# Edge tables by node made on ACT from destination rows, zero fills issued side by side, and a planner with other numbers, in a graph attention and mixture-of-experts kernel

## The chip, the cores and the metric

The kernel runs on one core of one Trainium2 chip. The metric is the device time in microseconds (us) of one launch; lower is better. Engines: PE multiplies matrices, DVE (vector), ACT (scalar, activation functions) and POOL (GpSimd, which here issues indirect gathers and scatters) work beside it, and SP issues the plain DMAs. Each engine takes its instructions in the order in which the program gives them.

## The reference, cut to what matters

6250 nodes of 256 values, 100,000 edges sorted by destination. A graph attention layer with eight heads, a feed-forward net per node, then a mixture of eight experts of which each node takes two.

```python
h = (xn @ W).reshape(N, HEADS, HEAD_DIM)
e = leaky_relu(a_src[src] + a_dst[dst], 0.2)
ee = exp(e - segment_max(e, dst)[dst])
alpha = ee / segment_sum(ee, dst)[dst]
agg = segment_sum(h[src] * alpha[:, :, None], dst)
out = layer_norm(agg + xn @ W_res + bias)
x = x + out + gelu_tanh(out @ ffn_w1 + ffn_b1) @ ffn_w2 + ffn_b2
...
logits = layernorm(x) @ Wr + br          # then softmax, the top two experts
x = x + sum of the two experts' weight * (gelu(xn_e @ W1[e] + b1[e]) @ W2[e] + b2[e])
```

## The kernel before

**Setup** (to L761) makes the products of all nodes, writes a table `tab_s` of node rows (256 values of h and 16 source factors) to DRAM, a table `tab_q` of the 16 destination factors per node, and from the edges' destination indices the columns `loct` (which of the 32 nodes of its window an edge belongs to) and `snloc` (which of 128 accumulator rows a window's node stands for).

**Edges.** The edges lie in 784 tiles of 128. Four windows of 32 nodes make a group; a group has m = 1, 2, 4 or 8 tiles per window, so the four windows' i-th tiles make one *edge step*. There are 110 groups (66 with m = 1) and 196 steps, taken from the highest nodes down, so the first 66 steps end a group each. The stages of a step run at different delays in iterations of the main loop:

```python
STAGES = ((sum_up, 6), (weigh, 3), (add_tiles, 4), (place, 4), (turn_spread, 1), (give, 2),
          (spread, 0), (add_nodes, 5), (fetch, 0))
```

- `fetch` (L824, POOL): four indirect gathers of `tab_s` rows into `gs` (four buffers).
- `spread` (L833, DVE): the table `oh` of edges by node, one where an edge (its partition) belongs to a node (32 columns per window). At a group's first step it also makes `qd` (L840, DVE): the destination factors `gd` of the four windows' nodes, multiplied with the mask `quad`, so that each window's factors stand in columns of their own and zeros beside them. `gd` is loaded for 32 groups at once (L808, SP).
- `turn_spread` (L846, PE): transposes `oh` into the PSUM tile `pt`; ACT copies it out as `oht` (L848), now nodes on partitions and edges in columns. The tile `pt` has one buffer and also serves the transposes of `turn` (L978, evicted by ACT at L985).
- `give` (L854, PE): `oht` times `qd` brings each edge its destination factors, `pz`.
- `weigh` (L862 to L866, DVE): the edges' weights, then the weighted rows `msg`.
- `add_tiles` (L881, PE): `oh` times `msg` sums the edges by node in `pl`; behind a group's last step ACT copies it out as `part` (L885).
- `place` (L899, DVE, once a group): `oh2`, the table that puts the window nodes at their accumulator rows.
- `add_nodes` (L906, PE) and `sum_up` (L917, DVE, twice): add the group into `acc_hi` or `acc_lo`.

**Everything else is tasks.** A *first unit* (25 of them) makes `xn @ W_res` plus biases and stores it; a *node unit* (25, two tiles of nodes each, the last a single tile) takes the summed edges, norms them, runs the feed-forward net, stores the new rows (`store_new`, L1106, SP) and chooses the experts; every two node units a *chunk* ranks their nodes per expert, and POOL scatters their rows into the experts' lists `xs` (L1396). A *block* (53, three of them half) loads 256 rows of one expert's list (`xb`, L1456) and its weights (`w1b`, `w2b`, `b2b`, L1447 to L1449, 2.2 MB), runs the expert's net (`turn` L978, `up` L993 with the eviction `ht` at L996, `down` L1003) and adds the result to the output by an indirect scatter (L1498, POOL). A node unit may start once the edges of its nodes are summed; a block once enough chunks are listed. Before the last chunk, `clear` (L1408, SP) writes 384 rows of zeros behind the end of each of the eight experts' lists, because the last blocks may be only partly filled.

**The order** is fixed when the program is built: each iteration of the main loop first emits the stages of the edge steps, then takes tasks from a list in order, as far as each engine's budget (in the planner's own cost units) and the tasks' dependences allow:

```python
ROOM = {"PE": 7.5, "DVE": 7.6, "ACT": 5.0, "POOL": 2.6, "SP": 1e9}
EDGES = {"PE": 1.3, "DVE": 2.0}
BEHIND = {"PE": 0.5, "DVE": 1.4}
ROOM_AFTER = {"PE": 7.7, "DVE": 7.0, "ACT": 7.0, "POOL": 5.2, "SP": 1e9}
```

`EDGES` is taken off for each step and `BEHIND` for one that ends a group; `ROOM_AFTER` holds once the edge steps are done. A task of another engine comes at least one iteration behind what it needs unless a gap is given. `turn_of` is the order of the blocks; the half blocks have the numbers 50 to 52.

Of the kernel before, what the change touches and what calls it, by code (L numbers as in the profile page):

```python
# [48 lines left out]
ALU = mybir.AluOpType  # L50
# [18 lines left out]
EDGES = {"PE": 1.3, "DVE": 2.0}  # L69
BEHIND = {"PE": 0.5, "DVE": 1.4}  # L70
ROOM_AFTER = {"PE": 7.7, "DVE": 7.0, "ACT": 7.0, "POOL": 5.2, "SP": 1e9}
# [151 lines left out]
def gnn_moe_kernel(  # L223
# [68 lines left out]
    NCW = -(-NW // P)  # L292
    DUMMY = NP
# [12 lines left out]
    for i in range(NS - NF):  # L306
        turn_of += [NF + i, NF - (NS - NF) + i]
# [23 lines left out]
    xt_d = dp.tile([NT, P, KD * P], F32, name="xt_d")  # L331
    xs = dp.tile([E * CAP + BT, DX], F32, name="xs")
# [13 lines left out]
    snloc = gp.tile([P, NQ], F32, name="snloc")  # L346
    here = gp.tile([P, 2, NQ], F32, name="here")
# [55 lines left out]

    quad = cp.tile([P, G], F32, name="quad")
    nc.vector.memset(quad, 0.0)
    for j in range(G):
        nc.vector.memset(quad[j * W32:(j + 1) * W32, j:j + 1], 1.0)
# [52 lines left out]
    with ExitStack() as actx:  # L460
# [96 lines left out]
        nc.vector.tensor_copy(srf, srow)  # L557
        ends = ap_.tile([P, 2, NCH], F32, name="ends")
# [69 lines left out]
        for j in range(G):  # L628
            q = slice(j * W32, (j + 1) * W32)
            nc.vector.tensor_scalar(sn[q], first[q, :, j], pcol[q], float(-j * W32), op0=ALU.add,  # L630
                                    op1=ALU.add)
        nc.vector.tensor_sub(sn, sn, kff)
        nc.vector.tensor_scalar(snloc, sn, float(P), float(-P), op0=ALU.is_ge, op1=ALU.mult)
        nc.vector.tensor_add(snloc, snloc, sn)
        nc.vector.tensor_sub(sn, first[:, :, 0], kff)
# [45 lines left out]

        nc.vector.memset(acc_hi[:, NT - KHI, :], 0.0)
# [100 lines left out]
    GC = P // G  # L783
# [13 lines left out]
    gds = {}  # L797

    def fetch_nodes(c):

        gq = bw.tile([P, W32 * 2 * H], F32, name="gq", bufs=1)
        nc.gpsimd.indirect_dma_start(
            out=gq, out_offset=None, in_=tab_q,
            in_offset=bass.IndirectOffsetOnAxis(ap=qrow[:, c:c + 1], axis=0))
        nc.sync.dma_start(tab_g[c * P:(c + 1) * P, :], gq)
        n = min(GC, NQ - c * GC)
        gd = bw.tile([P, GC, 2 * H], F32, name="gd")
        nc.sync.dma_start(gd[:, :n], tab_g[c * P:c * P + n * G, :].rearrange(  # L808
            "(g j) (r c) -> (j r) g c", j=G, r=W32))
        gds[c] = gd  # L810
# [18 lines left out]
    def spread(s):  # L829

        q, i = order[s]
        oh = bw.tile([P, G, W32], F32, name="oh", bufs=6)
        nc.vector.tensor_tensor(oh, jrow[:, None, :W32].to_broadcast([P, G, W32]),  # L833
                                step_tiles(s, loct)[:, :, None].to_broadcast([P, G, W32]),
                                op=ALU.is_equal)
        live[s, "oh"] = oh
        if i == 0:
            qd = bw.tile([P, G, 2 * H], F32, name="qd", bufs=3)
            gd = gds[q // GC][:, q % GC, :]
            nc.vector.tensor_tensor(qd, gd[:, None, :].to_broadcast([P, G, 2 * H]),  # L840
                                    quad[:, :, None].to_broadcast([P, G, 2 * H]), op=ALU.mult)
            live[q, "qd"] = qd

    def turn_spread(s):
        po = cps.tile([P, KD, 2 * P], F32, name="pt")
        nc.tensor.transpose(po[:, 0, :P], live[s, "oh"].rearrange("p j r -> p (j r)"), ident)  # L846
        oht = bw.tile([P, P], F32, name="oht")
        nc.scalar.activation(oht, po[:, 0, :P], AF.Copy)  # L848
        live[s, "oht"] = oht

    def give(s):

        pz = bps.tile([P, G * 2 * H], F32, name="pz", bufs=2)
        nc.tensor.matmul(pz, live.pop((s, "oht")), live[order[s][0], "qd"].rearrange(  # L854
            "p j c -> p (j c)"), start=True, stop=True)
        live[s, "pz"] = pz
# [38 lines left out]
    @behind_group  # L895
    def place(q):

        oh2 = bw.tile([P, P], F32, name="oh2")
        nc.vector.tensor_scalar(oh2, jrow[:, :P], snloc[:, q:q + 1], None, op0=ALU.is_equal)  # L899
        live[q, "oh2"] = oh2  # L900
# [9 lines left out]
    def sum_up(q):  # L910
# [4 lines left out]
        for b in range(2):  # L915
# [6 lines left out]
    STAGES = ((sum_up, 6), (weigh, 3), (add_tiles, 4), (place, 4), (turn_spread, 1), (give, 2),  # L922
              (spread, 0), (add_nodes, 5), (fetch, 0))
# [17 lines left out]
    pending = []  # L941
    held = set()

    def task(*a, **k):
        t = Task(*a, **k)
        pending.append(t)
        return t
# [243 lines left out]
    loads, turned, added, normed, chosen_, scattered = [], [], [], [], [], []  # L1191

    def node_unit(u):
        t0, n, _ = units[u]
        env = {"n": n}
        ld = task(lambda: load_nodes(t0, n, env), "SP", 0.0,
                  [(firsts[u], 0),
                   *[(d, 0) for d in back(turned, 2) + back(added, 2) + back(normed, 3)]])
        dv = task(lambda: divide(t0, n, env), "DVE", 0.85 * n, [ld])
# [17 lines left out]
        loads.append(ld)  # L1217
# [171 lines left out]
    placed = {u: [] for u in range(NT)}  # L1389
    between = cp.tile([P, 1], F32, name="between")  # L1390

    def scatter(u, j):
        t = units[u][0] + j
        n = rows(t)
        for k in range(2):
            st = nc.gpsimd.indirect_dma_start(  # L1396
                out=xs, out_offset=bass.IndirectOffsetOnAxis(ap=slots[k][:n, t:t + 1], axis=0),
                in_=xes[u // 2][:n, place_of(u) + j, :], in_offset=None)
            tc.add_to_no_dep_group("slots", st.ins)
            placed[u].append(st.ins)  # L1400
            tc.declare_no_dep(st.ins, group="slots", reason="each token has slots of its own")

            nc.gpsimd.memset(between, 0.0)

    def clear(e):

        r = nc.sync.value_load(endi[0:1, e:e + 1], min_val=0, max_val=E * CAP - 3 * P)
        nc.sync.dma_start(xs[bass.ds(r, 3 * P), :].rearrange("(p r) d -> p r d", r=3),  # L1408
                          blank[:, None, :].to_broadcast([P, 3, DX]))

    def chunk_tasks(us, final, before_final):
# [17 lines left out]
        for u in us:  # L1429
            scattered.append([task(lambda u=u, j=j: scatter(u, j), "POOL", 2.6,  # L1430
                                   [rk, ad, *[(d, 0) for d in cleared]])
                              for j in range(units[u][1])])
            sc += scattered[-1]
# [116 lines left out]
    EARLY = 10  # L1550
    final_list, there = [], None
    s, u, since, was_nodes = 0, 0, [], False

    with tc.manual_schedule():
        nc.sync.dma_start(xs[E * CAP:, :].rearrange("(p r) d -> p r d", r=2),
                          blank[:, None, :].to_broadcast([P, 2, DX]))
        while s < NG + LASTST or pending or u < len(units) or len(blocks) < NS:
            for g in range(s, min(s + EARLY, NG)):
                if order[g][0] // GC not in gds:
                    fetch_nodes(order[g][0] // GC)  # L1560
# [19 lines left out]
            while sum(t.cost for t in pending if t.eng == "PE") < QUEUE:  # L1580
                if (u < len(units) and units[u][2] <= s - LASTST
                        and not (ahead and was_nodes)):
                    was_nodes = True
                    node_unit(u)
                    since.append(u)
                    u += 1
                    if u % 2 == 0 or u == len(units):
                        chunk_tasks(since, u == len(units), u == len(units) - 1)
                        since = []
                elif ahead:  # L1590
# [55 lines left out]
```

## Time and profile before

| | us |
|---|---|
| median of 3 runs (lowest, highest) | 1924.65 (1918.36, 1925.77) |
| the profiled execution | 1919.82 |
| its span | 1917.9 |
| edge steps, first and last transpose of L846 | 122.1 to 1580.6 |
| first and last product of the experts' second layer finished (L1488) | 680.9 to 1903.4 |
| gathers of L824, 784 of them, mean of one | 1.041 |
| ACT table loads at L996, 41 of them, mean of one | 1.283 |

The page divides the span into 40 slices of 48 us; a digit is the busy share in tenths:

```profile
PE   4835787878777899999799999999999996898996
DVE  8836888877788757584755665546444351131010
ACT  3831233223222344344334434343434341442342
POOL 2027775755565767767677677777877772221222
```

PE fills up from the fourteenth slice on, when the first blocks run, and has a gap behind the edge steps (the slice with a 6, near 1600 us). In lists of groups, a line reads: source line, engine, operation, written tile <- read tiles, count | busy us, mean ns of one | idle us of the engine before them, and who ended it. In lists of waits: waiting engine and line <- whom it waited for: us in total, times, longest. Lines of the timeline give start, duration, engine, line and operation. Columns of the stage table: stretch, its length, then busy us (and instructions) of each engine, granted PE clock, busy share of the 16 DMA engines, GB/s.

### The profile page before, as it was taken

The numbers are of one execution on the slowest core, as the hardware profiler recorded it, in microseconds if no ns is written. First come the engines' busy times: TensorE is split into PE (matmuls) and PEld (weight loads), VectorE is DVE, ScalarE is ACT, GpSimd is POOL, SyncE is SP. The second block draws the span as 40 slices with busy tenths as digits, with TensorE's granted clock in tenths as the row PEclk, the third lists the DMA queues.
The fourth block names the chain that finished last, engine by engine and source line by source line (L and its number), as shares of the span: only waits on it lengthen the run. The fifth ranks groups of instructions, "written<-read, shape, count | busy, mean of one in ns | idle before, by whom it ended". The sixth has DMA issues, their size and how long they took to land. (4 is left out here: it accounts for less than half of the span.)

```text
span 1917.9 us, 28185 instructions
## 1 busy us (share of the span) xinstructions
PE 1614.6 (84%) x8479; PEld 1238.1 (65%) x8479; DVE 1080.1 (56%) x3972; ACT 700.6 (37%) x1585; POOL 1124.8 (59%) x1162
## 2 busy tenths in 40 slices
PE   4835787878777899999799999999999996898996
PEld 3523565655555677776577777767777774676885
DVE  8836888877788757584755665546444351131010
ACT  3831233223222344344334434343434341442342
POOL 2027775755565767767677677777877772221222
PEclk8967899988877899999999999999999997998998
DMA  4967665554445476666565666767578674737671
GB/s 127 296 204 221 202 197 151 161 160 135 140 134 167 139 211 172 169 199 166 160 189 155 204 193 178 230 181 237 178 226 251 182 210 151 234 72 236 185 223 31
DMA packets 246622, 347.86 MB, mean 181 GB/s; under 512 B 46033, under 2 KB 202865, under 8 KB 246460
## 3 DMA queue, kind: packets, MB, share of 16 engines
q1 hardware_dynamic: 184268, 203.16, 32.7%
q0 software_dynamic: 58880, 139.32, 28.1%
q10 hardware_dynamic: 3312, 3.48, 0.6%
q8 instruction: 70, 1.15, 0.2%
q14 instruction: 92, 0.75, 0.1%
HBM read 282.50 MB, written 67.26 MB: 182 GB/s over the span
## 5 line engine op out<-in xcount | busy, mean ns | idle before, releaser
L824 POOL DMA_INDIRECT gs<-tab_s,srce x784 | 816.5, 1041 | 371.0 <-issue 201.6
L993 PE MATMUL ph<-turned_in,w1b 128*128 128x256 f32 (+1 forms) x1696 | 386.5, 381 | 35.0 <-DMA w1b<-in_L_ffn_W_dram 19.2
L1003 PE MATMUL py<-w2b,ht 128*128 128x256 f32 x1648 | 375.0, 386 | 14.3 <-DVE lg L1135 7.3
L993 PEld LDWEIGHTS ph<-turned_in,w1b 128*128 128x128 f32 x1696 | 300.5, 192 | 99.6 <-ACT ht L996 32.5
L1003 PEld LDWEIGHTS py<-w2b,ht 128*128 128x128 f32 x1648 | 316.1, 194 | 59.7 <-DVE lg L1135 8.9
L1498 POOL DMA_INDIRECT out_dram<-yb,tos x103 | 171.9, 1669 | 245.4 <-ACT yb L1494 125.3
L996 ACT ACTIVATE ht<-ph,pc 128x256 f32<-128x256 f32 (+1 forms) x424 | 196.5, 468 | 257.7 <-PE ph L993 255.5
L866 DVE TENSOR_TENSOR msg<-gs,msg 128x1024 f32<-128x1024 f32 x196 | 240.3, 1226 | 6.7
L993 PE MATMUL ph<-turned_in,w_sb 128*128 128x256 f32 (+1 forms) x800 | 194.1, 396 | 11.9 <-ACT ht L996 11.3
L1003 PE MATMUL py<-w_sb,ht 128*128 128x256 f32 x784 | 187.7, 400 | 11.2 <-DVE lg L1135 10.5
L1488 DVE TENSOR_TENSOR yb<-py,b2b 128x512 f32<-128x512 f32 (+1 forms) x53 | 35.8, 675 | 266.5 <-PE py L1003 252.9
L1003 PEld LDWEIGHTS py<-w_sb,ht 128*128 128x128 f32 x784 | 156.6, 202 | 38.9 <-DVE lg L1135 14.7
L993 PEld LDWEIGHTS ph<-turned_in,w_sb 128*128 128x128 f32 x800 | 151.7, 201 | 42.7 <-ACT ht L996 16.2
L848 ACT ACTIVATE oht<-pt 128x128 f32<-128x128 f32 x196 | 53.9, 275 | 288.5 <-PE pt L846 257.5
L885 ACT ACTIVATE part<-pl 128x264 f32<-128x264 f32 x110 | 42.9, 390 | 313.3 <-PE pl L881 310.3
L996 ACT ACTIVATE ht<-ph,prm 128x256 f32<-128x256 f32 (+1 forms) x200 | 92.8, 470 | 124.7 <-PE ph L993 124.4
L1396 POOL DMA_INDIRECT xs<-xe,slot x98 | 104.8, 1069 | 56.7 <-DMA xs<-blank 28.0
L881 PE MATMUL pl<-msg,oh 128*32 128x264 f32 x1568 | 131.1, 406 | 5.1 <-DVE msg L866 5.0
L906 PE MATMUL p<-part,oh 128*128 128x264 f32 x220 | 85.0, 472 | 55.3 <-DVE acc_hi L917 37.1
L862 DVE TENSOR_TENSOR ww<-gs,pz 128x64 f32<-128x64 f32 x196 | 42.1, 215 | 158.5 <-PE pz L854 100.3
L846 PEld LDWEIGHTS pt<-ident,oh 128*128 128x128 f32 x196 | 27.7, 141 | 139.0 <-issue 85.0
L917 DVE SCALAR_TENSOR_TENSOR acc_lo<-p,here,acc_lo 128x264 f32 x112 | 55.2, 493 | 101.1 <-PE p L906 79.6
(334 smaller groups left out, 1925.7 us busy)
## 6 DMA issues: line engine op xcount, KB each, us to landing
w1b<-in_L_ffn_W_dram SPq DMA_DIRECT2D x53, 1024.0 KB
w2b<-in_L_ffn_W_dram SPq DMA_DIRECT2D x53, 1024.0 KB
xb<-xs SPq DMA_DIRECT2D x50, 260.0 KB
gs<-tab_s,srce POOLq DMA_INDIRECT x784, 3.5
b2b<-in_L_ffn_b_dram SPq DMA_DIRECT2D x53, 128.0 KB
tab_s<-hg SPq DMA_DIRECT2D x12, 544.0 KB
xg<-in_x_dram SPq DMA_DIRECT2D x12, 512.0 KB
xt_d<-xt SPq DMA_DIRECT2D x12, 512.0 KB
```

The lines of the kernel that those rows point to most:

```text
L824: nc.gpsimd.indirect_dma_start(out=gs[:, j, :], out_offset=None, in_=tab_s, in_offset=bass.IndirectOffsetOnAxis(ap=srce[:, t:t + 1], axis=0))
L848: nc.scalar.activation(oht, po[:, 0, :P], AF.Copy)
L866: nc.vector.tensor_tensor(msg[:, :, :D].rearrange("p t (h d) -> p t h d", h=H), gs[:, :, :D].rearrange("p t (h d) -> p t h d", h=H), msg[: ...
L881: nc.tensor.matmul(pl[j * W32:(j + 1) * W32, :], oh[:, j, :], msg[:, j, :], start=i == 0, stop=last)
L885: nc.scalar.activation(part, pl, AF.Copy)
L906: nc.tensor.matmul(p2, oh2, part, start=True, stop=True)
L917: nc.vector.scalar_tensor_tensor(to, p2, here[:, b, q:q + 1], to, op0=ALU.mult, op1=ALU.add)
L993: nc.tensor.matmul(ph[:, :W], w1[:, k, c * P:(c + 1) * P], env["in"][:, k, :W], start=k == 0, stop=k == KD - 1)
L996: nc.scalar.activation(ht[:, :W], ph[:, :W], func, bias=b[:, c:c + 1], scale=1.0)
L1003: nc.tensor.matmul(env["py"][:, j, :], env["ht", c][:, j * P:(j + 1) * P], w2[:, c, :], start=c == 0, stop=c == KF - 1)
L1396: st = nc.gpsimd.indirect_dma_start(out=xs, out_offset=bass.IndirectOffsetOnAxis(ap=slots[k][:n, t:t + 1], axis=0), in_=xes[u // 2][:n, pl ...
L1498: st = nc.gpsimd.indirect_dma_start(out=out, out_offset=bass.IndirectOffsetOnAxis(ap=tos[:, b, j:j + 1], axis=0), in_=env["yb"][:, j, :], ...
```

## The change

Six things change together.

1. `oht` is no longer a transpose. A new DRAM tile `dst_d` holds the destination index of each edge, a tile of edges per row (written once in setup). `load_dst` (SP) lays the four tiles' rows of a step onto the partitions of their windows, each row to 32 partitions, into `rows_` (four buffers), and `is_node` (ACT) makes the table from it: Relu(1 - |row - node|), with the partition's node in the column `node`. The delay of `spread` becomes 1, since only `add_tiles` reads `oh` now.
2. `qd` is no longer computed. Three buffers `qds` for four groups each are zeroed once; `fetch_factors` (SP) loads the four windows' factors into their columns with four DMAs for every four groups.
3. `place` makes `oh2` by `is_node` on ACT instead of a comparison on DVE.
4. The zero fills of `clear` are declared independent of each other and of scatters before them; scatters after them wait for them.
5. Planner: `EDGES` and `BEHIND` smaller, `ROOM_AFTER` halved, node loads a unit ahead, stores of new rows two iterations behind what they store, scatters rather than the normalizing wait for these stores, and the last node unit's tasks go to the front of the list.
6. The order of the last blocks: a full block ahead of each half one, so that a half block is last.

```diff
-EDGES = {"PE": 1.3, "DVE": 2.0}
-BEHIND = {"PE": 0.5, "DVE": 1.4}
-ROOM_AFTER = {"PE": 7.7, "DVE": 7.0, "ACT": 7.0, "POOL": 5.2, "SP": 1e9}
+EDGES = {"PE": 0.95, "DVE": 2.0}
+BEHIND = {"PE": 0.5, "DVE": 1.0}
+ROOM_AFTER = {"PE": 3.9, "DVE": 3.5, "ACT": 3.5, "POOL": 2.6, "SP": 1e9}
...
-        turn_of += [NF + i, NF - (NS - NF) + i]
+        turn_of += [NF - (NS - NF) + i, NF + i]
...
+        nc.sync.dma_start(dst_d.rearrange("(c t) e -> t c e", t=P), drf)
...
+    def fetch_factors(c):
+
         n = min(GC, NQ - c * GC)
...
+        for j in range(G):
+            nc.sync.dma_start(
+                qds[c % QB][j * W32:(j + 1) * W32, :n, j, :], bass.AP(
+                    tensor=tab_g.tensor,
+                    offset=tab_g.offset + (c * GC * G + j) * W32 * 2 * H,
+                    ap=[[2 * H, W32], [G * W32 * 2 * H, n], [1, 2 * H]]))
...
-        if i == 0:
-            qd = bw.tile([P, G, 2 * H], F32, name="qd", bufs=3)
-            gd = gds[q // GC][:, q % GC, :]
-            nc.vector.tensor_tensor(qd, gd[:, None, :].to_broadcast([P, G, 2 * H]),
-                                    quad[:, :, None].to_broadcast([P, G, 2 * H]), op=ALU.mult)
-            live[q, "qd"] = qd
-
-    def turn_spread(s):
-        po = cps.tile([P, KD, 2 * P], F32, name="pt")
-        nc.tensor.transpose(po[:, 0, :P], live[s, "oh"].rearrange("p j r -> p (j r)"), ident)
+
+    def load_dst(s):
+
+        q, i = order[s]
+        t0, m = groups[q]
+        rows_ = bg.tile([P, P], F32, name="rows_")
+        nc.sync.dma_start(rows_, bass.AP(tensor=dst_d.tensor, offset=dst_d.offset + (t0 + i) * P,
+                                         ap=[[m * P, G], [0, W32], [1, P]]))
+        live[s, "rows"] = rows_
+
+    def is_node(out, rows_, less):
+
+        nc.scalar.activation(out, rows_, AF.Abs, bias=less)
+        nc.scalar.activation(out, out, AF.Relu, bias=1.0, scale=-1.0)
+
+    def spread_by_node(s):
+
+        q, i = order[s]
         oht = bw.tile([P, P], F32, name="oht")
-        nc.scalar.activation(oht, po[:, 0, :P], AF.Copy)
+        is_node(oht, live.pop((s, "rows")), node[:, q:q + 1])
         live[s, "oht"] = oht
...
-        nc.vector.tensor_scalar(oh2, jrow[:, :P], snloc[:, q:q + 1], None, op0=ALU.is_equal)
+        is_node(oh2, jrow, snloc[:, q:q + 1])
...
-    STAGES = ((sum_up, 6), (weigh, 3), (add_tiles, 4), (place, 4), (turn_spread, 1), (give, 2),
-              (spread, 0), (add_nodes, 5), (fetch, 0))
+    STAGES = ((sum_up, 6), (weigh, 3), (add_tiles, 4), (spread_by_node, 1), (place, 4), (give, 2),
+              (spread, 1), (add_nodes, 5), (load_dst, -1), (fetch, 0))
...
+                          [(firsts[u], 0), *[(d, 0) for d in back(turned, 2) + back(added, 2)
+                                             + back(normed, 3) + back(stores, 3)]]))
...
-        st = task(lambda: store_new(t0, n, env), "SP", 0.0, [tk])
+        stores.append(task(lambda: store_new(t0, n, env), "SP", 0.0, [(tk, 2)]))
...
-                  [nn, (st, 0), *[(d, 0) for d in free]])
+                  [nn, *[(d, 0) for d in free]])
...
+            for i in blanks:
+                tc.add_manual_dep(st.ins, i.name, mybir.DependencyInfo(
+                    mybir.DependencyClass.Sync, mybir.DependencyReason.DATA),
+                    reason="the zeros come first")
...
+        st = nc.sync.dma_start(xs[bass.ds(r, 3 * P), :].rearrange("(p r) d -> p r d", r=3),
+                               blank[:, None, :].to_broadcast([P, 3, DX]))
+        for i in blanks + [i for u in placed for i in placed[u]]:
+            tc.declare_no_dep(st.ins, i, reason="no rows of other tokens or experts")
+        blanks.append(st.ins)
...
+                    if u == len(units) - 1:
+                        urgent.append(0)
+                    if u not in loaded:
+                        loaded[u] = node_loads(u)
+                    node_unit(u, loaded[u])
                     since.append(u)
                     u += 1
+                    if u < min(len(units), len(firsts)):
+                        loaded[u] = node_loads(u)
```

More of the change, by code (lines that the diff above doesn't have):

```diff
@@ L292, in gnn_moe_kernel @@
     NCW = -(-NW // P)
+    GC = 4
+    QB = 3
     DUMMY = NP
@@ L331, in gnn_moe_kernel @@
     xt_d = dp.tile([NT, P, KD * P], F32, name="xt_d")
+    dst_d = dp.tile([NCH * P, P], F32, name="dst_d")
     xs = dp.tile([E * CAP + BT, DX], F32, name="xs")
@@ L346, in gnn_moe_kernel @@
     snloc = gp.tile([P, NQ], F32, name="snloc")
+    node = gp.tile([P, NQ], F32, name="node")
+    qds = [gp.tile([P, GC, G, 2 * H], F32, name=f"qd{i}") for i in range(QB)]
     here = gp.tile([P, 2, NQ], F32, name="here")
@@ L402, in gnn_moe_kernel @@
     nc.gpsimd.iota(number, pattern=[[P, NT]], base=0, channel_multiplier=1)
[L404 to L407, printed above, removed]
     prm = cp.tile([P, NPR], F32, name="prm")
@@ L631, in gnn_moe_kernel @@
                                     op1=ALU.add)
+        nc.vector.tensor_scalar(node, sn, -1.0, None, op0=ALU.mult)
         nc.vector.tensor_sub(sn, sn, kff)
@@ L634, in gnn_moe_kernel @@
         nc.vector.tensor_add(snloc, snloc, sn)
+        nc.vector.tensor_scalar(snloc, snloc, -1.0, None, op0=ALU.mult)
         nc.vector.tensor_sub(sn, first[:, :, 0], kff)
@@ L680, in gnn_moe_kernel @@
         nc.vector.tensor_scalar(srce, stmp, float(DUMMY), None, op0=ALU.add)
+        for qd in qds:
+            nc.vector.memset(qd, 0.0)
         nc.vector.memset(acc_hi[:, NT - KHI, :], 0.0)
@@ L780, in gnn_moe_kernel @@
     fb2_bc = bcast(ffn_b2[None, :], "fb2_bc", D, fp)
-    GC = P // G
     cw = gnn.enter_context(tc.tile_pool(name="cw", bufs=2))
@@ L796, in gnn_moe_kernel @@
     live = {}
-    gds = {}
+    fetched = [0, 0]
     def fetch_nodes(c):
@@ L805, in fetch_nodes @@
         nc.sync.dma_start(tab_g[c * P:(c + 1) * P, :], gq)
+    def fetch_factors(c):
         n = min(GC, NQ - c * GC)
[L807 to L810, printed above, removed]
+        for j in range(G):
[4 more added lines that the diff above has]
+                    ap=[[2 * H, W32], [G * W32 * 2 * H, n], [1, 2 * H]]))
     def step_tiles(s, a):
@@ L829, in spread @@
     def spread(s):
-        q, i = order[s]
-        oh = bw.tile([P, G, W32], F32, name="oh", bufs=6)
+        oh = bw.tile([P, G, W32], F32, name="oh", bufs=5)
         nc.vector.tensor_tensor(oh, jrow[:, None, :W32].to_broadcast([P, G, W32]),
@@ L853, in give @@
         pz = bps.tile([P, G * 2 * H], F32, name="pz", bufs=2)
-        nc.tensor.matmul(pz, live.pop((s, "oht")), live[order[s][0], "qd"].rearrange(
-            "p j c -> p (j c)"), start=True, stop=True)
+        q = order[s][0]
+        qd = qds[q // GC % QB][:, q % GC]
+        nc.tensor.matmul(pz, live.pop((s, "oht")), qd.rearrange("p j c -> p (j c)"), start=True,
+                         stop=True)
         live[s, "pz"] = pz
@@ L939, in __init__ @@
             self.step = None
-    pending = []
+    pending, urgent = [], []
     held = set()
@@ L945, in task @@
         t = Task(*a, **k)
-        pending.append(t)
+        if urgent:
+            pending.insert(urgent[0], t)
+            urgent[0] += 1
+        else:
+            pending.append(t)
         return t
@@ L1189, in first_unit, with node_loads, node_unit @@
         firsts.append(task(lambda: store_first(t0, n, env), "SP", 0.0, [ab]))
-    loads, turned, added, normed, chosen_, scattered = [], [], [], [], [], []
-    def node_unit(u):
+    stores, loads, turned, added, normed, chosen_, scattered = [], [], [], [], [], [], []
+    def node_loads(u):
         t0, n, _ = units[u]
         env = {"n": n}
[L1196 to L1199, printed above, removed]
+        loads.append(task(lambda: load_nodes(t0, n, env), "SP", 0.0,
+                          [(firsts[u], 0), *[(d, 0) for d in back(turned, 2) + back(added, 2)
+                                             + back(normed, 3) + back(stores, 3)]]))
+        return env
+    def node_unit(u, env):
+        t0, n, _ = units[u]
+        dv = task(lambda: divide(t0, n, env), "DVE", 0.85 * n, [loads[u]])
         no = task(lambda: norm_out(n, env), "DVE", 0.6 * n + 1.9, [dv])
@@ L1216, in node_unit @@
         ch = task(lambda: choose(t0, n, env), "DVE", 0.65 * n, [lo], free="py")
-        loads.append(ld)
         turned.append(turns[-1])
@@ L1387, in enlist @@
             nc.vector.tensor_copy(endi, start)
-    placed = {u: [] for u in range(NT)}
+    placed, blanks = {u: [] for u in range(NT)}, []
     between = cp.tile([P, 1], F32, name="between")
@@ L1407, in clear @@
         r = nc.sync.value_load(endi[0:1, e:e + 1], min_val=0, max_val=E * CAP - 3 * P)
-        nc.sync.dma_start(xs[bass.ds(r, 3 * P), :].rearrange("(p r) d -> p r d", r=3),
-                          blank[:, None, :].to_broadcast([P, 3, DX]))
+        st = nc.sync.dma_start(xs[bass.ds(r, 3 * P), :].rearrange("(p r) d -> p r d", r=3),
[3 more added lines that the diff above has]
+        blanks.append(st.ins)
     def chunk_tasks(us, final, before_final):
@@ L1430, in chunk_tasks @@
             scattered.append([task(lambda u=u, j=j: scatter(u, j), "POOL", 2.6,
-                                   [rk, ad, *[(d, 0) for d in cleared]])
+                                   [rk, ad, (stores[u], 0), *[(d, 0) for d in cleared]])
                               for j in range(units[u][1])])
@@ L1550, in gnn_moe_kernel @@
     EARLY = 10
+    NCG = -(-NQ // GC)
     final_list, there = [], None
-    s, u, since, was_nodes = 0, 0, [], False
+    s, u, since, was_nodes, loaded = 0, 0, [], False, {}
     with tc.manual_schedule():
@@ L1557, in gnn_moe_kernel @@
         while s < NG + LASTST or pending or u < len(units) or len(blocks) < NS:
-            for g in range(s, min(s + EARLY, NG)):
-                if order[g][0] // GC not in gds:
-                    fetch_nodes(order[g][0] // GC)
+            while fetched[0] < NCW and order[min(s + EARLY, NG - 1)][0] // 32 <= NCW - 1 - fetched[0]:
+                fetch_nodes(NCW - 1 - fetched[0])
+                fetched[0] += 1
+            while (fetched[1] < NCG
+                   and order[min(s + EARLY - 4, NG - 1)][0] // GC <= NCG - 1 - fetched[1]):
+                fetch_factors(NCG - 1 - fetched[1])
+                fetched[1] += 1
+            if s == 0:
+                load_dst(0)
             for f, d in STAGES:
@@ L1583, in gnn_moe_kernel @@
                     was_nodes = True
-                    node_unit(u)
+                    if u == len(units) - 1:
[3 more added lines that the diff above has]
+                    node_unit(u, loaded[u])
                     since.append(u)
                     u += 1
+                    if u < min(len(units), len(firsts)):
+                        loaded[u] = node_loads(u)
                     if u % 2 == 0 or u == len(units):
@@ L1589, in gnn_moe_kernel @@
                         since = []
+                    urgent.clear()
                 elif ahead:
```

## Prediction

> **What bounds the kernel now.** I read the page's engine totals first, then a table of stages that I cut where the work changes: setup to 122 us, start of the edge steps, edge steps without expert blocks (to about 650), edge steps with blocks (to 1600), the stretch around the last node unit, the last blocks.
>
> ```profile
> span 1917.9 us, 28185 instructions
> PE 1614.6 (84%) x8479; PEld 1238.1 (65%) x8479; DVE 1080.1 (56%) x3972; ACT 700.6 (37%) x1585; POOL 1124.8 (59%) x1162
> ```
>
> ```profile
> core 0: us, PE busy (x) PEld busy (x) DVE busy (x) ACT busy (x) POOL busy (x), PEclk, DMA share, GB/s
> 122.00:250.00 128.00, 74.84 (x384) 50.98 (x385) 82.47 (x229) 22.18 (x58) 93.28 (x83) 0.75 0.73 212
> 250.00:650.00 400.00, 315.99 (x1600) 230.03 (x1599) 321.27 (x1178) 118.48 (x271) 242.61 (x270) 0.85 0.53 157
> 650.00:1600.00 950.00, 881.69 (x4915) 680.93 (x4914) 537.25 (x1863) 379.68 (x820) 703.63 (x681) 0.98 0.65 190
> 1600.00:1750.00 150.00, 111.79 (x506) 92.20 (x506) 28.93 (x139) 45.40 (x94) 33.73 (x32) 0.88 0.60 178
> ```
>
> From 650 to 1600 PE is busy 93%; DVE and ACT are far below. POOL's 703.6 us needs its 0.3 us of issue between two instructions added (681 x 0.3 = 204): 907 of 950, so POOL stands close behind PE. From 250 to 650 nothing is full by its busy share, so I asked who waits for whom, there and in the next stage:
>
> ```profile
> PE p L906 <- DVE acc_hi L917: 26.1, 11, 4.8
> PE p L906 <- DVE acc_lo L917: 18.0, 6, 7.0
> ...
> PE pt L846 <- ACT turned_in L985: 4.0, 9, 0.5
> ```
>
> ```profile
> POOL gs L824 <- DVE msg L866: 94.8, 32, 9.0
> ```
>
> PE and POOL both wait for DVE in this stage, and DVE has 1178 small instructions in 400 us: DVE sets its pace. In the block stage PE waits for ACT alone:
>
> ```profile
> PE ph L993 <- ACT ht L996: 21.4, 23, 1.8
> PE pt L846 <- ACT turned_in L985: 18.3, 28, 2.3
> ```
>
> **PE: the transpose goes.** Its busy time (196 x 336 ns = 65.9 us) overstates it. In the timeline of a step it starts 0.16 us before the product that follows it (438.29 against 438.45); with and without it, the steps' edge instructions take 0.92 and 0.86 us. So it is worth 0.065 to 0.165 us; I take 0.115 us x 127 steps of the block stage = 15 us. It also shares one PSUM tile with the blocks' turns and so waits for their eviction: 18.3 us, which vanish with it. What is late next is the same blocks' eviction before the next turn, already counted in other rows. Block stage: -33 us.
>
> **DVE: two operations per group go.**
>
> ```profile
> L899 DVE TENSOR_SCALAR oh<-jrow,snloc 128x128 f32<-128x128 f32 x110 | 30.9, 281 | 0.0
> L840 DVE TENSOR_TENSOR qd<-gd,quad 128x64 f32<-128x64 f32 x110 | 23.9, 217 | 20.2 <-DMA gd<-tab_g 20.2
> L996 ACT ACTIVATE ht<-ph,prm 128x128 f32<-128x128 f32 x8 | 2.8, 367 | 1.5 <-PE ph L993 1.3
> L848 ACT ACTIVATE oht<-pt 128x128 f32<-128x128 f32 x196 | 53.9, 275 | 288.5 <-PE pt L846 257.5 <-DMA tab_g<-gq 19.9 <-PE pl L881 8.0
> ```
>
> They overlap their neighbours, so I count from start to start: 0.20 us and about 0.15 us (443.55, 443.75, 443.95, 444.08). From 250 to 650 each of some 52 steps ends a group: 52 x 0.35 = -18 us, since DVE sets the pace there. Later, DVE is 57% busy and the gain is nothing.
>
> **ACT: an eviction goes, two pairs come.** Abs with a bias from a column, then Relu, per step and again per group: 306 pairs. The nearest rows are 367 ns (128x128 with such a bias) and 275 ns (plain copy). The second reads the first's result, so no overlap: 0.55 to 0.80 us a pair, and I take 0.74 (two of the first row). ACT gains 306 x 0.74 - 53.9 = 173 us and comes to about 46% of the span. In a step that ends no group, the pair waits for nothing of that step and runs while PE finishes the step before. In one that ends a group it stands behind the eviction of `part`, which waits for PE, and the evictions of `ht` stand behind it. PE can fill two `ph` tiles first, 1.74 us; ACT needs 0.2 + 0.39 + 2 x 0.74 + 0.47 = 2.5 us after the sums, PE 0.3 + 0.5 + 1.74 = 2.5. The cover just suffices; 44 ends at 0 to 0.5 us: +8 us (0 to 22). Here a rule speaks against the change: the Trainium skill, ScalarE: Activation LUTs, Rules for kernel authors, would put Relu and the like on VectorE. By operation cost it is right: 1.48 us on ACT for the two pairs of a group end against 0.28 us on DVE and 0.28 on ACT, 130 us more for 110 groups. But ACT is 30% busy where DVE sets the pace, so I charge only PE's waits. That Abs needs no table load of 1283 ns is not in this trace (it shows Copy and Identity without one); the same page, Table sets, lists abs and relu in every set. I charge nothing.
>
> **SP and DMA.** Each step adds a load of 128 rows of 512 B, and each four groups four loads of 64-byte pieces in place of their share of `gd` (the piece count stays). The trace's 512-byte packets on SP's queue took 28 ns: 196 x 128 x 28 ns over 16 DMA engines is 2.3% of the span. The Trainium skill, DMA: Bandwidth & Descriptors, Rules for kernel authors, says that a source whose outermost dimension is 4 runs on at most 4 engines: a load then takes 32 x 28 = 0.9 us, not 0.2. Either is small beside the lead: a row load issued in step s is read by ACT in s + 2, two steps (14 us) later. Ahead of it on the queue can be one block's 2.4 MB, which at the stage's 190 GB/s are 13 us; but those loads belong to the step before and wait for PE's products, so SP passes them about a step early. Cover holds by some 6 us; I charge 3 us for misses (0 to 150). SP issues cost 0.37 to 0.48 us, two per step: free. Factor loads wait for the product that last read their buffer, one step back, and the row load stands behind them; it keeps more than a step. At the start, row loads stand behind twelve factor loads, about 5 us of issue, and the first product comes later by 4 us (it waited 20.2 us for `gd`); setup gains 1 us of DVE work. Start: +5 us (0 to 10).
>
> **Planner's numbers.** PE's room for tasks rises by 0.35 per step. In about 129 steps that is 45 units, 2.9 blocks at 15.4 units, moved from behind the edges to beside them; it costs there what it saves later (about 41 us), since PE is the bound in both. Node units start at the step that the edges' progress allows (unit 13 at step 76, allowed at 75), so they don't move. Stores a step later, node loads a unit earlier, the last unit first: SP's long waits for the stored rows held up little but the tail.
>
> **The tail.**
>
> ```profile
> 1590.52 23.63 SPq L1408 DMA_DIRECT2D xs<-blank  x8
> 1616.87 0.39 SPq L1456 DMA_DIRECT2D xb<-xs  x1
> 1618.05 0.37 SPq L1447 DMA_DIRECT2D w1b<-in_L_ffn_W_dram  x1
> ```
>
> Eight zero fills run one after the other, 3.2 us each, and the next block's loads stand behind them on SP; PE stood 19.2 us before the block of 1625. Side by side they take 8 issues (about 5 us) and 8 x 384 packets x 52 ns / 16 = 10 us on the rings: PE's wait falls to about 7 us, -12. Scatters on POOL that come after them still wait those 10 us. The other 19 us of PE's idling from 1600 to 1750 lie around the last node unit, whose chain runs from 1633 to 1724 in steps of 8 us; half steps and the front place shorten it, but three more blocks are then done, and of the 37 that can be listed before the last-but-one chunk of nodes is routed hardly one is left to fill the wait: -6 us (-15 to +10). A half block at the end gives one output scatter instead of two: -3. Tail: -21.
>
> **Sum.** +5 - 18 - 33 + 8 + 3 - 21 = -56 us. The profiled execution took 1919.8 us (span 1917.9 and 1.9 around it): 1864. The runs' median lies 4.8 us above it; I forecast 1866.
>
> **Rivals.**
> - *Rows arrive late (slower).* If block loads ahead on the queue leave a row load 13 us behind and SP is not a step early, ACT stands, in order, and `ht`, then PE with it. It decides once landing takes more than two steps, about 14.6 us. With 5 us at each of 35 blocks' loads: +175 less the 3: about 2035; with half of it 1950. For it: SP blocked up to 6.6 us in one issue in the tail. Against: its waits in the block stage end with PE's products.
> - *POOL becomes the bound.* It needs 907 us plus three more blocks' scatters (about 12) in the block stage; PE after the change needs 950 - 22 + 41 = 969 there. Only if DMA work stretches the gathers (1041 ns mean, 950 at best) by another 100 ns over 520 gathers does POOL hold the steps; the gain is then -18, -21, +5: about 1890.
> - *More is freed.* DVE's stage shortens with its queue (waits for `msg`, 94.8 us), and PE never starves in the tail: 1825.
> - *It eats itself up.* ACT stalls at their upper bound and the tail starves for listed blocks: 1864 + 14 + 16 + 20 = about 1915.
>
> **Chances and numbers.** The sum as above 0.55 (1840 to 1890), POOL 0.15, more freed 0.12, eaten up 0.05, late rows 0.13. A measurement here can tell 0.5% from no change, about 10 us. Faster 0.78, same 0.09, slower 0.13. The range, 1815 to 1935, leaves out most of the late rows and the best of the freed case.
>
> **What would show it.** Right: PE's waits for `pt` of the step gone; the stage from 250 to 650 some 18 us shorter in the same steps; ACT near 875 us without more table loads; the eight fills within 12 us; about 37 blocks done when the edges end. Wrong: ACT waiting for the row tile by more than a few us, PE's wait for `ht` in the block stage above 45 us, or PE idle over 40 us after the edges.

## The result, and the profile after

| | before | after |
|---|---|---|
| median of 18 runs each, side by side (lowest, highest) | 1921.21 (1912.78, 1925.80) | 1907.89 (1896.54, 1914.34) |
| ratio, 95% interval | 1 | 0.9931 (0.9916 to 0.9945) |
| profiled execution: span | 1917.9 | 1906.2 |

The change brings 13 us where 56 were forecast: direction right, size not. The totals of the page of the changed kernel:

```profile
span 1906.2 us, 28325 instructions
PE 1596.4 (84%) x8283; PEld 1227.4 (64%) x8283; DVE 1046.0 (55%) x3752; ACT 835.7 (44%) x2000; POOL 1121.2 (59%) x1162
```

PE does 196 products less and is as full as before; ACT took 135 us on (forecast 173), without more table loads at `ht` (40). Now the table of stages, cut as before:

```profile
core 0: us, PE busy (x) PEld busy (x) DVE busy (x) ACT busy (x) POOL busy (x), PEclk, DMA share, GB/s
122.00:250.00 128.00, 67.25 (x319) 45.18 (x320) 67.88 (x175) 35.84 (x100) 80.69 (x80) 0.69 0.76 220
250.00:650.00 400.00, 326.44 (x1644) 242.42 (x1644) 319.92 (x1129) 176.25 (x439) 260.15 (x279) 0.87 0.57 169
650.00:1600.00 950.00, 880.60 (x4817) 679.10 (x4815) 518.94 (x1753) 449.26 (x1035) 702.95 (x683) 0.98 0.72 205
1600.00:1750.00 150.00, 107.61 (x496) 90.01 (x497) 27.43 (x134) 45.02 (x93) 29.34 (x28) 0.83 0.50 148
```

The last row is the surprise: behind the edges PE is not fuller than before (107.6 of 150 us, against 111.8), though that is where -62 us were forecast to show (-21 and the 41 of three blocks moved away). By stretches of work instead of fixed times, each from one profile (every step writes one `ww`, its edges' weights, on DVE):

| us | before | after | forecast |
|---|---|---|---|
| first `ww` | 143.6 | 153.3 | +5 |
| step 10 to step 60 | 390.0 | 380.1 | -18 |
| step 60 to last `ww`, and blocks done by then | 992.1, 33 | 1003.5, 36 | +19 (-22, and 41 for three blocks) |
| last `ww` to the end of the span (the tail) | 332.7 | 309.5 | -62 |

Up to the last `ww` the sum is 11.5 us late against a forecast of 6. Of the 44 us missed by the two profiles, 39 are in the tail. Its one long wait of PE, from the timeline of PE and that of SP's queue:

```profile
1693.75 0.39 PE L1315 MATMUL py<-m,ones 128*128 128x32 f32 x2
1729.09 1.12 PE L1003 MATMUL pt<-ident,xb 128*128 128x128 f32 x4 [34.96 <-DMA xb<-xs]
```

```profile
1705.39 0.39 SPq L1482 DMA_DIRECT2D w1b<-in_L_ffn_W_dram  x1
1705.97 0.38 SPq L1483 DMA_DIRECT2D w2b<-in_L_ffn_W_dram  x1
1706.54 0.50 SPq L1484 DMA_DIRECT2D b2b<-in_L_ffn_b_dram  x1
...
1709.22 4.77 SPq L1484 DMA_DIRECT2D b2b<-in_L_ffn_b_dram  x1
...
1717.17 4.30 SPq L1484 DMA_DIRECT2D b2b<-in_L_ffn_b_dram  x1
1722.30 8.31 SPq L1491 DMA_DIRECT2D xb<-xs  x4
```

PE has finished all 41 blocks that can be listed without the last node unit. The last list, which tells the other twelve blocks their expert and their rows, is ready at 1704.3 (DVE); the first weights leave at 1705.4, but the tokens `xb` of the next block only at 1722.3, behind the weights of three blocks. The zero fills themselves are what the forecast wanted (23.63 us before):

```profile
1578.42 11.59 SPq L1440 DMA_DIRECT2D xs<-blank  x8
```

### The profile page after: what moved, and what is told of

Its sections match the earlier page's. It is cut to its first block, busy times and chain, and to the rows that moved or that the text cites. A ratio compares the mean times of both kernels' runs of the same rounds, so it can differ in the third digit from the quotient of the medians.

```text
span 1906.2 us, 28325 instructions
## 1 busy us (share of the span) xinstructions
PE 1596.4 (84%) x8283; PEld 1227.4 (64%) x8283; DVE 1046.0 (55%) x3752; ACT 835.7 (44%) x2000; POOL 1121.2 (59%) x1162
## 5 line engine op out<-in xcount | busy, mean ns | idle before, releaser
L836 POOL DMA_INDIRECT gs<-tab_s,srce x784 | 814.6, 1039 | 364.3 <-issue 203.5
L875 PEld LDWEIGHTS pz<-qd,oht 128*128 128x128 f32 x392 | 60.9, 195 | 120.6 <-issue 109.8
L875 PE MATMUL pz<-qd,oht 128*128 128x64 f32 x392 | 88.1, 307 | 32.9 <-DMA rows__1882<-dst_d 32.9
```

The lines of the kernel that those rows point to most:

```text
L836: nc.gpsimd.indirect_dma_start(out=gs[:, j, :], out_offset=None, in_=tab_s, in_offset=bass.IndirectOffsetOnAxis(ap=srce[:, t:t + 1], axis=0))
L875: nc.tensor.matmul(pz, live.pop((s, "oht")), qd.rearrange("p j c -> p (j c)"), start=True, stop=True)
```

## The experiments

My theory after the result: the tail is not a sum of PE's work but a chain, last `ww`, last node unit, last list, first loads, twelve blocks. Blocks done earlier don't shorten it, and the queue ahead of `xb` lengthens it. Rivals: the tables bring nothing, or the tail's edits don't. All ratios below are to the kernel before on the same chip.

**First four: pieces.** On that chip the kernel before took 2117.87 us.

```
e1_tables:   edits 1 to 3; planner, fills, unit and block order as before
e2_tail:     edits 4 to 6 with the old EDGES and BEHIND; edge tables as before
e3_room:     the change with EDGES PE 1.3 and BEHIND DVE 1.4
e4_xb_first: the change, and for the last twelve blocks (i > 40)
+            env["lx"] = task(lambda: load_block(b, env), "SP", 0.0, [*needs, *free])
-                         [needs[-1], *[blocks[j] for j in user]])
+                         [needs[-1], *[blocks[j] for j in user], (env["lx"], 0)])
```

> Only the tables of edges change (parts 1 to 3); the zero fills, the planner's numbers and order, the stores and the order of the last blocks are as before. Theory 'tail' (the edge steps gained, and the gain was lost while PE waits for the last blocks to be listed): start +10 us, edge steps -10 and about -30, tail as before, so about 1890 us against 1921 (-25 to -35), with 33 or 34 blocks done when the edge steps end. Rival 'tables' (the ACT pairs and the row loads cost what the transpose and the DVE operations cost): within 6 us of the kernel before, the gain of the change coming from its tail parts alone.

> Only the tail parts change (zero fills side by side, node loads ahead, stores later, last unit first, halved budgets behind the edges, half block last); tables and the budgets beside the edges as before. Theory 'tail': 33 blocks at the end of the edges, so four to five listed ones are left and PE does not starve for long; 15 to 25 us faster than before (1896 to 1906). Rival 'tables': all of the change's 13 us come from here, 1908.

> The changed kernel with the former budgets beside the edge steps (EDGES, BEHIND). Theory 'tail': about three blocks fewer done when the edges end, edge steps some 40 us shorter, the wait for the last listed blocks under 15 us instead of 35; in all 10 to 20 us faster than the changed kernel, about 1893. Rival 'room' (more tasks beside the edges is right, the wait has another cause): the same 35 us of waiting and 1908 or slower.

> The changed kernel, but of the last twelve blocks each one's rows are loaded ahead of its weights, not three blocks' weights ahead of the first rows. Theory 'tail': of the 35 us wait 10 lie before the list is made and 25 behind it; the latter fall to about 12, so PE waits 20 to 24 us and the time is about 1895. Rival: the rows wait for the scatters, not for the weights in front of them; the wait stays above 30 us and the time at 1908.

Measured: 1.0025 (0.9993 to 1.0058), 0.9957 (0.9934 to 0.9979), 1.0041 (1.0015 to 1.0067), 0.9988 (0.9963 to 1.0014). None of the four came to the time that its theory gave (e1 came to that of its rival, e3 went the other way), and nothing adds up to 0.993. The change itself was not run on that chip, so it and three of these were put side by side on another. The chips of the next two groups took 1920 and 1923 us for the kernel before.

**The change and three pieces on one chip.**

> The kernel after itself, on the same chip as the three next to it, because the first four edits ran on a chip where the kernel before took 2118 us. If what the change brings belongs to the program, the ratio to before is again 0.993 within 0.003 on any chip; if it belongs to the chip (the first four pieces added up to about nothing there), it is 0.997 or more wherever before takes about 2118 us.

> Tables, rows and factors alone (no room, no tail edits), once more beside the whole change. Theory 'tables speed the edges': the last step's weights are formed 25 to 30 us earlier with 33 blocks done, and the end follows: 0.986. Rival 'tables pay for themselves': what PE no longer does comes back as waits for ACT in the block stage, so 1.000 within 0.003, as on the first chip.

> The whole change but with the planner's old room in the edge stage (1.3 and 1.4 instead of 0.95 and 1.0), so about two blocks move back behind the edges. Theory 'the tail is a chain': from the last step the end is the last node unit's chain, the first load and twelve blocks, so two blocks moved behind the edges fill PE's wait and the edges end up to 28 us earlier: 0.980. Rival 'work is work': PE's wait stays and the blocks are only later, within 0.003 of the whole change.

> The whole change, but for the twelve blocks listed last the tokens are loaded ahead of the weights instead of behind three blocks' weights. Theory 'PE waits for a queued load': the 35 us wait for xb falls to about 20 and the end comes 12 to 15 us earlier: 0.986. Rival 'the weights are the limit': PE then waits for w1b instead and the end moves by less than 4 us: 0.992.

Measured: f1 0.9930 (0.9903 to 0.9958), f2 0.9942 (0.9917 to 0.9966), f3 0.9893 (0.9873 to 0.9913), f4 0.9881 (0.9846 to 0.9915). The change repeats. The tables bring less than half of what f2's first theory said. f3 and f4 both lie below the 0.9916 to 0.9945 first measured for the change, though their intervals overlap that of f1 a little: its own new room seems to cost time, and so does the queue. f3 gained less than a third of what its theory said, since PE still waited 20.1 us for `xb`. In f4 the order on SP's queue and PE's waits are these:

```profile
1704.99 0.39 SPq L1491 DMA_DIRECT2D xb<-xs  x1
1706.39 0.38 SPq L1482 DMA_DIRECT2D w1b<-in_L_ffn_W_dram  x1
```

```profile
1708.24 1.12 PE L1003 MATMUL pt<-ident,xb 128*128 128x128 f32 x4 [14.45 <-DMA xb<-xs]
1717.42 1.08 PE L1003 MATMUL pt<-ident,xb 128*128 128x128 f32 x4 [8.07 <-DMA xb<-xs]
```

One wait of 35 us became two of 14.5 and 8.1, and the span is 13.7 us below that of the changed kernel's profile above, as the first theory expected (by the ratios of f1 and f4, 9 us).

**What queues xb, the two edits together, the start, and DVE in place of ACT.**

```
g1_room_after:  the change with the old ROOM_AFTER (POOL 5.2, and so on)
g2_room_xb:     f3 and f4 together
g3_rows_first:  g2, and load_dst(0), load_dst(1) ahead of fetch_factors at s == 0
g4_dve:         g2, and in is_node (node and snloc no longer negated)
-        nc.scalar.activation(out, rows_, AF.Abs, bias=less)
-        nc.scalar.activation(out, out, AF.Relu, bias=1.0, scale=-1.0)
+        nc.vector.tensor_scalar(out, rows_, less, None, op0=ALU.is_equal)
```

> The whole change, but with the old room behind the edges (POOL 5.2 a step instead of 2.6, and so on). In the changed kernel one give-back of 2.6 uses up POOL's room of a step, so the last scatters, on which the first xb waits, are issued a step behind the list, and three blocks' weights stand ahead of xb on SP's queue. Theory 'halved room queues xb': with the old room the order is weights, xb, weights again, the 35 us wait falls to 20 to 24 and the end comes 8 to 13 us earlier: 0.987. Rival 'order of the deps, not the room': SP's order stays as it is and the time stays within 0.002 of the whole change, 0.993.

> The whole change with the planner's old room in the edge stage (two blocks more behind the edges) and xb ahead of the weights for the last twelve blocks. Theory 'the tail is a chain': the last list comes 4 to 8 us earlier than with the new room and the end 174 us after it, so 1870 to 1874 us: 0.975. Rival 'one gain only' (either edit removes the same 35 us wait): no better than the better of the two alone, 0.988.

> As the one with the old room and xb first, and besides the rows of the first two steps are loaded ahead of the twelve loads of factors. Theory 'SP's queue makes the late start': the first weights are formed 6 us earlier and the end moves by as much: 0.972. Rival 'the start waits for the factors anyway': the first PE work on edges waits for the factors' DMA in place of the rows', 0 to 2 us.

> As the one with the old room and xb first, but both tables come from one DVE comparison each (is_equal with the node number, as the kernel before made the second of them) instead of two ACT operations. Theory 'ACT's pair delays ht': PE's waits for ACT in the block stage (ht and turned_in, about 50 us) fall to about 40 and the edge stage loses 5 us of DVE time, net -5 to 0 us. Rival 'DVE sets the pace of the edge stage': 86 more comparisons of 0.28 us there cost up to 24 us in steps 10 to 60, so +5 to +15 us.

Measured: g1 0.9876 (0.9849 to 0.9904), g2 0.9840 (0.9820 to 0.9861), g3 0.9850 (0.9829 to 0.9871), g4 0.9902 (0.9882 to 0.9922).

- g1: my reason for the queue falls. SP's order is the same, three blocks' weights and then four `xb`, and PE waits 34.9 us. The order follows from the plan's dependences: a weight load needs only the list and a free buffer (L1550), `xb` also the last scatter (L1552), an iteration later. With all listed blocks finished, three weight buffers are free at once. In f2 one set of weights went ahead of the first `xb`, in f3 two. So the queue is the price of running out of listed blocks. g1, on another chip, is still half a per cent ahead of f1; its tail is 4 us shorter, and the rest I can't trace.
- g2: the best version on these chips, 1891.56 us in the median; by the ratios both edits count (f3 0.9893, f4 0.9881), though less than the 0.975 of the theory.
- g3: the first `ww` comes 5 us sooner, but steps 10 to 60 take 392 us instead of 385, and the time doesn't fall. The start was no loss that could be had back this way.
- g4: the comparison on DVE costs 18.7 us in steps 10 to 60 (403.6 against 384.9) and takes 5.7 less from step 60 on (973.9 against 979.6). The second is no finding: f3, whose PE and ACT do the same work in the same order as those of g2 there, took 987.3. The table of stages, first g2, then g4:

```profile
250.00:650.00 400.00, 324.11 (x1605) 239.72 (x1604) 318.44 (x1110) 172.36 (x429) 258.53 (x273) 0.85 0.56 168
```

```profile
250.00:650.00 400.00, 313.07 (x1542) 229.86 (x1542) 322.83 (x1144) 105.55 (x216) 240.36 (x261) 0.85 0.56 164
```

DVE is as full in both (318, 323), and PE and POOL get less done: DVE does set the pace there. Some 102 comparisons at the prediction's 0.20 us from start to start are 20.4 us, and 18.7 were paid.

**Undoing one edit of g2.** This chip (2120.5 us before) and the next (2114.5) were like the first.

```
h0_room_xb:       g2
h1_fills_in_turn: g2, fills and scatters dependent on each other as before
h2_unit_in_turn:  g2, last node unit, node loads and stores as before
h3_pe_turns:      g2 without edits 1 to 3 (PE's transpose, qd and oh2 on DVE)
i1_pe_turns, i2_fills_in_turn: h3 and h1 again, on the second of these chips
```

> The version with the planner's old room in the edge stage and xb ahead of the weights once more, as the reference for the three next to it. 0.984 within 0.002 again.

> As the reference, but the eight zero fills wait for each other and for the scatters again, as in the kernel before. Theory 'the fills hold SP's queue ahead of listed blocks' loads': the wait for w1b of 19 us at about 1600 us is back, but since listed blocks run out before the list comes, most of it only moves PE's later wait for xb: +2 to +5 us. Prediction's own price for it, if nothing else hides it: +12 us.

> As the reference, but the last node unit queues behind the listed blocks, its loads and its store in the old places. Theory 'the list decides the end': the chain from the last step to the list grows from about 118 to about 141 us, as in the kernel with the tables alone, and PE's wait shrinks as more blocks lie ahead: +8 to +14 us. Rival (the prediction's price, range -10 to +15): +6 us at most, since the blocks that now run in that time are not run later.

> The kernel before with the edits of the tail and xb first, old room in the edge stage: no tables on ACT, PE turns the destination table again. Theory 'the tables are worth what PE is rid of': 17 to 22 us slower than the reference (18 us of PE time by the two profiles, and the waits at those turns), 0.994. Rival 'tables cancel themselves': within 5 us of the reference, 0.986.

> The version with xb first and the planner's old room, but with no tables on ACT (PE turns the destination table, DVE makes the second one), once more, since on the chip of the last four runs, where the kernel before took 2120 us, it was 0.4% ahead of its sister with the tables. On a chip where the kernel before takes about 1920 us, its sister with the tables was 0.984. Theory 'tables are worth what PE is rid of, where nothing else stalls': 0.990 to 0.994 (11 to 19 us slower than the sister). Rival 'tables cancel themselves on every chip': 0.982 to 0.986.

> The version with xb first and the old room, but the eight zero fills wait for each other and for the scatters again, once more beside the other. Its sister was 0.984. Theory 'the list decides the end': the fills only delay listed blocks that PE reaches too early anyway, 0 to +5 us: 0.984 to 0.987. The prediction's own price of the fills, if nothing hides it: +12 us, 0.990.

Measured: h0 1.0006 (0.9979 to 1.0034), h1 1.0015 (0.9987 to 1.0043), h2 1.0133 (1.0092 to 1.0174), h3 0.9969 (0.9941 to 0.9997); i1 0.9958 (0.9931 to 0.9984), i2 1.0075 (1.0039 to 1.0111). What the tables are worth beside the tail's edits where the kernel before takes 1920 us, the question of i1, is thus not measured. The ratios scatter here, but the tail, free of edge steps, takes the same time on both kinds of chip (g2 308.0 us, h0 308.6). Cut at the last list, it reads off the pieces:

| tail, us | blocks done | last `ww` to list | list to end | sum |
|---|---|---|---|---|
| before | 33 | 143.0 | 189.8 | 332.7 |
| f2 (tables) | 33 | 141.5 | 189.2 | 330.7 |
| f3 (old room) | 34 | 118.6 | 195.8 | 314.4 |
| after | 36 | 107.6 | 201.9 | 309.5 |
| f1 (after again) | 36 | 103.8 | 202.1 | 305.9 |
| g1 (old room behind the edges) | 36 | 103.4 | 198.4 | 301.8 |
| f4 (xb first) | 36 | 107.6 | 188.6 | 296.2 |
| g2 (both) | 34 | 118.8 | 189.2 | 308.0 |
| h0 (g2) | 34 | 120.1 | 188.5 | 308.6 |
| h1 (fills in turn) | 34 | 133.6 | 188.5 | 322.1 |
| i2 (fills in turn) | 34 | 134.1 | 188.3 | 322.4 |
| h2 (unit in turn) | 33 | 138.1 | 189.6 | 327.7 |

From list to end it is 188 to 190 us for every kernel, unless two (196) or three (202, in g1 198) sets of weights stand ahead of `xb`. The rest is when the list comes. In turn, the fills delay the list by 13.5 us (h1; 14.0 in i2), as much as PE waits again for weights, with the last node unit's products behind that wait. First the kernel before, then h1:

```profile
PE ph L993 <- DMA w1b<-in_L_ffn_W_dram: 19.2, 1, 19.2
```

```profile
PE ph L1018 <- DMA w1b<-in_L_ffn_W_dram: 13.7, 1, 13.7
```

In the tail, then, the prediction's own price holds, and the expectation that I wrote for h1 falls. The whole time does not show it on that chip (h1 1.0015, h0 1.0006, a difference within the noise); i2, on the next, is at 1.0075 without g2 beside it. The last unit's place, undone together with the early node loads and the later stores, is worth 18 us of the list (h2), more than was given for it; the three were not parted.

## Why the prediction missed, step by step

Two steps failed: waits that the tables remove were counted as time won, and blocks moved beside the edges were expected to cost nothing in sum. Taken one after the other by the ratios (times 1921 us): tables 0.9942, -11; edits of the tail on top with the queue out of the way (g2 against f2), -20; the new room (f4 against g2), +8; the queue (f1 against f4), +9. By the spans of the single profiles they are -20, -12, +6 and +14. Taken so, the terms must add up to the change, so their sum confirms nothing. f2 and f4 ran on another chip than g2, and by the intervals each term is good to 5 to 9 us, so room and queue are barely clear of none; that both cost time is read from the tails above. The forecast had -35 for the tables, -21 for the tail, and nothing for room and queue: of the 43 us missed, 24 are the tables' and 17 those of room and queue by the ratios, 15 and 20 by the spans.

- **The tail, -21, was about right and then taken back.** Fills 12 forecast, 13.5 measured on the list; last unit 6, measured 18 with its loads and stores; the half block at the end 3, of which nothing is seen (from PE's last product to the end 14.7 us before, 14.9 after). The step that failed is the planner's: "it costs there what it saves later (about 41 us), since PE is the bound in both". Behind the edges PE isn't the bound alone; the list is. Two blocks more beside the edges (f4 against g2) put the last `ww` 18.0 us later and bring the list only 11.2 us nearer to it, and from the list on both take the same. And with five listed blocks left instead of eight, PE runs dry at 1694 and three sets of weights go ahead of `xb`, 13 us (201.9 against 188.6). The prediction saw that hardly a listed block would be left to fill the wait, but priced it inside a range (-15 to +10) and didn't ask in which order SP issues the loads then. That was "eats itself up" in the tail alone: its time, 1915, had more ACT stalls in it, which didn't come. Its wrong sign was named: PE idle over 40 us after the edges; it waited 35 for `xb` and 6 for `w1b`.
- **The tables, -35 with start and rows, brought -11 (the profile of f2, one of its faster executions, shows -18 at the last `ww`).** From step 60 to the last `ww` f2 takes 16.7 us less. Of PE's own 15 us most are there: its busy time falls by 12.7 (from 910.8 to 898.1). The 18.3 us of waits at the transpose are gone as rows, but not as time: PE's idle time in that stretch falls by 4.0 only (from 81.3 to 77.3). PE's waits from 650 to 1600, two more rows of the kernel before and then f2:

```profile
PE pt L978 <- ACT turned_in L985: 16.9, 14, 1.5
PE py L1003 <- DVE lg L1135: 7.3, 3, 5.9
```

```profile
PE ph L1018 <- ACT ht L1021: 23.7, 21, 2.9
PE pt L1003 <- ACT turned_in L1010: 18.7, 15, 2.3
PE py L1028 <- DVE lg L1160: 14.8, 7, 6.7
PE pl L902 <- DVE msg L887: 4.5, 3, 1.6
```

  `ht` (21.4 before), `turned_in`, `lg` and `msg` took up most of what the transpose gave. "What is late next is already counted in other rows" was the error: those rows grew.
- **DVE's stage, -18:** -9.9 us in steps 10 to 60, -8.7 in f2 (-8.6 and -9.6 in the mean of cuts up to five steps earlier or later). g4 shows that DVE work counts there in full, so some of what was removed lay beside another wait already; which, is not shown.
- **ACT, +8:** PE's wait for `ht` (31.3 us) stayed below 45, but no run parts this term from the scatter of single profiles (g4 and f3 above). One sum of the prediction is wrong: two pairs at 1.48 us against 0.28 on DVE and 0.28 on ACT are 101 us more for 110 groups, not 130; nothing was charged for it. The rule of the Trainium skill (ScalarE: Activation LUTs, Rules for kernel authors) that Relu and the like belong on VectorE was put to the test by g4, with one comparison on DVE for each pair: in this kernel it loses 0.6% (0.9902 against 0.9840), since DVE is the pace of the first stage.
- **Start, +5:** +9.7; the row loads left SP behind the twelve factor loads as foreseen, and setup ended 4.5 us later (its last eviction `hg` at 121.4 against 116.9).
- **Late rows, POOL:** neither came. ACT waited for row tiles only at the start, gathers took 1039 ns as before (1041), and PE, not POOL, is full in the block stage. In the trace of the change a row load that stands alone takes 1.3 us from its first packet to its last (median of 139, the shortest 0.8), which is nearer to the 0.9 than to the 0.2 of the prediction.

## What to carry to other kernels

Behind a stage that ends with a routing decision, cut the time at that decision: work moved ahead of it pays only if the decision comes earlier by as much, and work held back is the cover that hides the wait for it. When a change eats into that cover, look at what the queues will issue first once the wait ends. And a wait that vanishes on an engine is a gain only after the sum of all of that engine's waits has been seen to fall.

## What the runs showed of the hardware

Chips differ by 10% for this program: 1920 us on the chip of the result and on those of the f and g kernels, 2115 to 2120 on the three of the e, h and i kernels. Single operations are hardly slower there (gathers 1024 ns in h0, 1042 in g2; first-layer products 392 and 383, at a mean granted clock of 0.893 and 0.925), nor are the tail or setup; the edge steps are (step 60 to the last: 979.6 us in g2, 1150.3 in h0, the same program). Waits of h0 from 700 to 1500, and one line of its timeline:

```profile
POOL gs L836 <- DVE oh L844: 117.3, 38, 7.0
...
PE ph L1018 <- ACT ht L1021: 43.3, 21, 12.0
...
PE ph L1018 <- issue: 24.4, 18, 5.5
```

```profile
1199.09 0.60 ACT L1007 ACTIVATE turned_rt<-pt 128x512 f32<-128x512 f32 x1 [15.67 <-remote]
```

In g2 the first of the waits is 26.3 us and the last of them doesn't occur. ACT stood 15.7 us before the eviction of the last line, though the transposes that it reads had ended at 1186.6, and the profile names no work of the kernel that held it (`remote`); PE then waited 12.0 us for ACT. What holds the engines stays open. On those chips the tables bring nothing (e1 1.0025) or cost a little (h0 1.0006 against h3 0.9969), and g2 gains nothing, so the 0.984 holds for the faster chips alone; the change itself (0.993) was run on no other.

In the tails SP stood 3.2 to 6.4 us in an issue whenever a second or third set of weights was issued close behind the first (4.77 and 4.30 us above, 5.67 and 3.44 in f3, where the same load mostly takes 0.35 to 0.5 us), so what stands behind weights on that queue waits for more than its place.
